# A two-layer graph network kernel: 70 early gathers, finishes by pairs of groups, one-hots made two groups ahead, and a share of the last weighted rows on GpSimd

## Chip, cores and metric

The kernel runs on one core of a Trainium2 chip, in a single launch. The metric is the device time of one execution in microseconds (us). Before the change the median of 10 runs is 2741.71 us (2734.19 to 2759.88). The core's engines are called PE (matmul), DVE (vector), ACT (scalar activation), POOL (GpSimd, which here issues the gathers) and SP (which issues the plain transfers).

## What is computed

The graph has N = 6250 nodes with 256 features (D) and 106,250 edges sorted by target, with self loops and two relations. Layer 0 sends along each edge a two-step message of the source node (a different weight for each relation), sums the messages by target, puts the sums through a gated update and a small network, adds the input and normalizes. Layer 1 is graph attention with 4 heads (H) of 64, followed by two more residual normalizations.

```python
S = feat[src]
for r in range(2):
    msgs = where(rel == r, relu(relu(S @ W_rel[r].T + b) @ W_rel[r].T + b), msgs)
agg = segment_sum(msgs, dst)
i, f, g, o = split(agg @ W_ih.T + b_ih + b_hh, 4)
hn = sigmoid(o) * tanh(sigmoid(i) * tanh(g))
x = layernorm(x + mlp(hn))
...
h = (x @ W).reshape(n, H, F)
e = leaky_relu(a_src[src] + a_dst[dst], 0.2)
ex = exp(e - segment_max(e, dst)[dst])
out = segment_sum(h[src] * (ex / (segment_sum(ex, dst)[dst] + 1e-16)), dst) + bias
y = relu(layernorm(out + x) * gamma + beta)
x = layernorm(x + y)
```

## The kernel before

**Tiling.** The edges other than self loops, in target order, are cut into TC = 782 tiles of 128. Seven tiles make a window (WT = 7, NW = 112 windows), two windows a group of 128 target nodes (NG = 56 groups of 14 tiles). A group's sums also use the first tile of the next group (GS = 15 tiles), since a tile's edges can run over the border. A segment sum over a group is a chain of matmuls into one PSUM bank: a one-hot matrix (edge by target) against the edge rows. `one_hot` builds a group's one-hots with three DVE instructions (L1835).

**Front.** The lists are made and both relations' messages are computed once for every source node, in blocks, and stored to the DRAM table `parts0`. After the block before BLOCK1 = 26 and the one before BLOCK2 = 39, POOL gathers the first edge rows early (L1606): `ahead_tiles` lists KEPT1 = 3 tiles of each of the first AHEAD_W = 12 windows for the first batch and KEPT2 = 2 for the second, 60 in all. The row buffers `G` are a ring of ten, seven tiles each, which the gathers of both layers use.

**Stage 0 (layer 0).** `order` goes through all other tiles, one gather a step (L1718, table `parts0`). LAG = 4 steps behind, `sum0` issues the matmul of that tile (L2178). When a group's sums are complete, DVE makes `kind` and `agg` from them (L1927, L1931), and for each four groups `update` runs gates, network and layer norm (the normalization's statistics end at L2062) and writes rows for layer 1. AHEAD_G are the groups whose windows had early gathers; their one-hots and first sums are issued ahead of the loop.

**Holds.** `Pace` remembers for every step the last DVE instruction traced so far. `Pace.hold` lets every fourth gather wait for the DVE instruction of the step `ahead` steps back: AHEAD0 = 6 steps in stage 0, AHEAD1 = 4 in stage 1, where an extra lead is given that falls from 42 steps to none over the first 250 tiles and grows again over the last 42. The instructions of an engine run in the order in which the program traces them; there is no other scheduling. `Steps` holds coroutines ("chains") that are advanced once a step; a `yield k` puts the rest off by k steps.

**Stage 1 (layer 1).** Groups are handled in 26 pairs, and the last four one by one (`pairs`). In order of a pair's life:

- `ahead`: for each group a DVE one-hot `ohT` (L2351), PE products `pn` that fetch the target's logits (L2365), and a DVE reduction `of` (L2369); also the segment borders `cut`, turned by PE and copied by ACT.
- `weights`: ACT has copied the logits from the gathered rows (L2642, L2651); PE turns them (L2392), DVE runs two scans (L2399, L2400), PE and ACT pass the ends between tiles (L2403 to 2405), DVE adds logits (L2406, L2407) and runs two more scans (L2409, L2410), PE turns back (L2415), DVE takes the maxima (L2418 to 2421), ACT exponentiates into PSUM `bank` (L2423).
- `weighted`: called by `sum1` for each window piece; makes the group's one-hots if they are not there, then `gw`, the rows times their weights (L2438 and L2444 on DVE, L2443 on ACT). A seven-tile piece is 128x1792 elements. Four `gw` buffers.
- `sum1`: the matmul of one tile into the group's PSUM sum `fps1`, of which there are two (L2564). With the first sum of an even group, SP loads `k3` (kept rows of two groups). With a group's last sum the chain `finish` starts.
- `finish` for one group: subtract, exponential (L2462, L2464, ACT L2465), denominator (L2468 to 2472), the own row and the sums (L2479, L2482), scaling and residual (L2485, L2486), `normed(0)` (L2494, L2495, ACT L2496/2497, DVE L2499, ACT L2502), weight, offset and relu (L2506 to 2508), `normed(1)`, store. The last group also moves rows by a matmul (L2518, L2526).

In the loop each step has one gather (from t = EARLY = 21 on; the first 21 are made between the stages), one or two calls of `sum1`, one `run.step()` and one `pace.passes()`.

Of the kernel before, what the change touches and what calls it, by code (L numbers as in the profile page):

```python
# [33 lines left out]
F32 = mybir.dt.float32  # L34
# [8 lines left out]
P = 128  # L43
# [3 lines left out]
H = 4  # L47
# [22 lines left out]
GS = 2 * WT + 1  # L70
LOW, MID = P // 2, (WT, WT + 3)
# [9 lines left out]
AHEAD_W = 12  # L81
# [7 lines left out]
AHEAD1 = WT - 3  # L89
# [1551 lines left out]
def fast(  # L1641
# [164 lines left out]
    rings = {("G", id(rowsp)): [list(bufs), -(-len(soon) // WT)]}  # L1806
# [43 lines left out]
    with (  # L1850
# [17 lines left out]
        b1c = l0w.tile([P, 1], F32, name="fb1c")  # L1868
        b2c = l0w.tile([P, 1], F32, name="fb2c")
# [337 lines left out]
        seven = bufs[len(soon) // WT].rearrange("p (j f) -> p j f", f=HA)  # L2207
        pace = Pace(len(soon))
        for n in range(len(soon), TC + LAG):
            if n < TC:  # L2210
# [17 lines left out]
                pace.hold(move, n, AHEAD0)  # L2228
# [30 lines left out]
    with (  # L2259
# [8 lines left out]
        vec_p = vps.tile([P, 2, D], F32, name="vec_p")  # L2268
        nc.scalar.copy(vec_p, vec)
# [9 lines left out]
        def complete(t):  # L2279
# [9 lines left out]
            more = ring(eps, [P, D + 2 * H], F32, "fps1", 2)[:, :HA]  # L2289
# [15 lines left out]
        def ahead(pair, box):  # L2305
# [25 lines left out]
            else:  # L2331
                o = pair[0] % 2 * GS * H
                n = ((len(pair) - 1) * GS + len(tiles_in(pair[-1])[1])) * H
                pc = ring(tps, [P, P + 1], F32, "turn", 2)
# [8 lines left out]
            yield 12 if len(pair) > 1 else 8  # L2343
            for i, g in enumerate(pair):
                halves = node2[g % 4]
                for h, ps in enumerate((low_s, high_s)):
                    nc.scalar.copy(
                        halves[ps, h, :], node3[ps, g, :, :].rearrange("p c a -> p (c a)")
                    )
                ohT = ring(ep, [P, MID[1], P], BF16, "ohT", 2)  # L2350
                nc.vector.tensor_scalar(  # L2351
                    ohT.rearrange("p j e -> p (j e)"), dB[:, i, :], iota_p, None, op0=OP.is_equal
                )
                yield 2
                n = len(tiles_in(g)[1])
                pn = ring(ops, [P, GS, 3, 2 * H], F32, "pn", 2)
# [20 lines left out]
        def weights(pair, box):  # L2377
# [13 lines left out]
            pe = ring(tps, [P, P + 1], F32, "turn", 2)[:, :P]  # L2391
# [10 lines left out]
            pd = ring(tps, [P, P + 1], F32, "turn", 2)[:, :P]  # L2402
# [11 lines left out]
            pm = ring(tps, [P, P + 1], F32, "turn", 2)[:, :P]  # L2414
# [16 lines left out]

        def weighted(g, w, o, n, of, ex, top):

            if g not in ohs:
                ohs[g] = ring(ep, [P, (2 * WT - 2) * LOW + 3 * P], F32, "oh1", 2)
                one_hot(ohs[g], g, slot, MID[1])
# [7 lines left out]
            made = nc.vector.tensor_mul(  # L2444
                gw[:, :, :D].rearrange("p j (h f) -> p j h f", h=H),
                of[:, :n, :D].rearrange("p j (h f) -> p j h f", h=H),
                ex[:, o : o + n, :, None].to_broadcast([P, n, H, F]),
# [7 lines left out]
        def finish(g, ps):  # L2455
            u = everyone
            n = u.stop
            at_w = lows_of([g])
            k3 = k3s[g // 2][:, g % 2, :, :]
            sm = ring(fp, [P, 4, H], F32, "sm", 3)  # L2460
            w_own, den = sm[u, 0, :], sm[u, 1, :]
            nc.vector.tensor_sub(w_own, loop[u, g, :], ps[u, HA:])  # L2462
# [7 lines left out]
                den, ps[u, D:HA], 1e-16, w_own, op0=OP.add, op1=OP.add  # L2470
            )
            nc.vector.reciprocal(den, den)
            yt = ring(fp, [P, D], F32, "fy", 3)
            y = yt[u, :]

            def heads(ap):
                return ap.rearrange("p (h f) -> p h f", h=H)

            nc.vector.tensor_mul(  # L2479
                heads(y), heads(k3[u, 2, :]), w_own[:, :, None].to_broadcast([n, H, F])  # L2480
            )
            nc.vector.tensor_add(y, y, ps[u, :D])  # L2482
            read.add(g)
            yield 1
            nc.vector.tensor_mul(heads(y), heads(y), den[:, :, None].to_broadcast([n, H, F]))  # L2485
            nc.vector.tensor_add(y, y, k3[u, 1, :])  # L2486
            yield 1
            mv = ring(fp, [P, 2, 2], F32, "fmv1", 3)
            rs = ring(fp, [P, 2, 2], F32, "frs1", 3)

            def normed(k):
                st = ring(fp, [P, nc.vector.BN_STATS_DIM], F32, "fst1", 3)
                r, m = rs[u, k, 0:1], rs[u, k, 1:2]
                nc.vector.bn_stats(st[u, :], y)  # L2494
                nc.vector.bn_aggr(mv[u, k, :], st[u, :])  # L2495
                nc.scalar.activation(r, mv[u, k, 1:2], AF.Ln, bias=eps_c[u])  # L2496
                nc.scalar.activation(r, r, AF.Exp, scale=-0.5)
                yield 2
                nc.vector.scalar_tensor_tensor(  # L2499
                    m, mv[u, k, 0:1], -1.0, r, op0=OP.mult, op1=OP.mult  # L2500
                )
                nc.scalar.activation(y, y, AF.Identity, bias=m, scale=r)  # L2502
# [3 lines left out]
            nc.vector.tensor_mul(y, y, vec_p[u, 0, :])  # L2506
            nc.vector.tensor_add(y, y, vec_p[u, 1, :])
            nc.vector.scalar_tensor_tensor(y, y, 0.0, k3[u, 0, :], op0=OP.max, op1=OP.add)
            yield 1
            yield from normed(1)  # L2510
            in_order(written, g)
            if g in at_w:
                nc.sync.dma_start(out[bass.ds(at_w[g], P), :], yt)
            results[g] = yt
            if g == NG - 1:
                moved = ring(eps, [P, D + 2 * H], F32, "fps1", 2)[:, :D]
                for q in range(2):
                    nc.tensor.matmul(  # L2518
                        moved,
# [202 lines left out]
```

## Time and profile before

| what | us |
|---|---|
| median of 10 runs | 2741.71 |
| profiled execution | 2747.18 |
| its span | 2745.3 |
| front, to the first gather of stage 0 | 257.8 |
| stage 0, to its last groups | 257 to 1422, POOL busy 712.5, DVE 372.9, PE 836.4 |
| change of stages | 1422 to 1500 |
| stage 1, to its last gather | 1500 to 2668, POOL busy 697.1, DVE 731.2, PE 526.7 |
| tail, without gathers | 2668 to 2745, DVE busy 52.1, PE 35.4 |
| L1718, 722 gathers of stage 0 | 693.5, 961 ns each |
| L1718, 761 gathers of stage 1 | 726.8, 955 ns each |
| L1606, 60 early gathers | 58.8 |
| L2444, 167 pieces `gw` | 249.0 |
| L2564, 1674 sums of stage 1 | 462.6 |

A line of a timeline has the start, the duration, engine, source line, operation, output and inputs, the count, and in brackets the idle time of that engine before it and what ended it. "Issue" there means that the profile shows no wait; "remote" and "another core or an unknown queue" that the releaser could not be found. A line of waits has the waiting instruction, what released it, the total in us, how often, and the longest. PE's ends in the records are modelled.

### The profile page before, as it was taken

The numbers are of one execution on the slowest core, as the hardware profiler recorded it, in microseconds if no ns is written. First come the engines' busy times: TensorE is split into PE (matmuls) and PEld (weight loads), VectorE is DVE, ScalarE is ACT, GpSimd is POOL, SyncE is SP. The second block draws the span as 40 slices with busy tenths as digits, with TensorE's granted clock in tenths as the row PEclk, the third lists the DMA queues.
The fourth block names the chain that finished last, engine by engine and source line by source line (L and its number), as shares of the span: only waits on it lengthen the run. The fifth ranks groups of instructions, "written<-read, shape, count | busy, mean of one in ns | idle before, by whom it ended". The sixth has DMA issues, their size and how long they took to land.

```text
span 2745.3 us, 21961 instructions
## 1 busy us (share of the span) xinstructions
PE 1624.4 (59%) x6113; PEld 877.7 (32%) x6113; DVE 1312.4 (48%) x3627; ACT 510.4 (19%) x1650; POOL 1538.5 (56%) x1610
## 2 busy tenths in 40 slices
PE   8956877657677677678744454453534435353444
PEld 5634433323333333234432322221322223122222
DVE  8642333223233232234322567575665757566557
ACT  3311121111211112112230111111111111111112
POOL 1534656556656666665545555555656566665650
PEclk9978988878888988789876766676767666666766
DMA  4334434434444344443424444434435354443440
GB/s 145 128 118 145 138 113 140 128 93 134 144 136 136 106 133 135 134 133 124 133 89 117 119 116 122 126 107 119 126 112 141 107 134 120 126 133 106 120 120 27
DMA packets 153969, 335.04 MB, mean 122 GB/s; under 512 B 37114, under 2 KB 74848, under 8 KB 153837
## 3 DMA queue, kind: packets, MB, share of 16 engines
q0 software_dynamic: 76048, 207.99, 27.3%
q1 hardware_dynamic: 75613, 122.50, 14.1%
q10 hardware_dynamic: 2176, 3.05, 0.3%
q8 instruction: 50, 0.82, 0.1%
q14 instruction: 82, 0.67, 0.1%
HBM read 280.89 MB, written 52.52 MB: 121 GB/s over the span
## 4 chain that ended last, share of the span: by engine, by line
PE 27%; DVE 25%; another core or an unknown queue 23%; issue 12%; ACT 5%; POOL 2%; DMA 2%; DVEq 0%; ACTq 0%; SPq 0%; POOLq 0%
PE fps L2178 10%; DVE gw L2444 6%; PE fpg L2009 5%; DVE oh L1835 3%; PE fps L2564 3%; POOL G L1718 2%; PE fpm L1572 2%; PE fpg L2095 1%; PE fph L1558 1%; DVE fst L2494 1%; DVE ohT L2351 1%; PE fps L2291 1%; PE fpg L2057 1%; DMA G<-parts,fidx 1%
## 5 line engine op out<-in xcount | busy, mean ns | idle before, releaser
L1718 POOL DMA_INDIRECT G<-rows,fidx x761 | 726.8, 955 | 489.7 <-issue 232.4
L1718 POOL DMA_INDIRECT G<-parts,fidx x722 | 693.5, 961 | 463.6 <-issue 202.5
L2178 PE MATMUL fps<-G,oh 128*64 128x257 f32 (+1 forms) x1674 | 499.8, 433 | 133.2 <-ACT G L2224 53.7
L2564 PE MATMUL fps<-gw,oh 128*64 128x264 f32 (+1 forms) x1674 | 462.6, 464 | 186.0 <-DVE gw L2444 165.7
L2178 PEld LDWEIGHTS fps<-G,oh 128*64 128x64 f32 (+1 forms) x1674 | 223.5, 164 | 382.3 <-issue 190.8
L2564 PEld LDWEIGHTS fps<-gw,oh 128*64 128x64 f32 (+1 forms) x1674 | 238.8, 175 | 331.2 <-DVE gw L2444 173.5
L2444 DVE TENSOR_TENSOR gw<-G,bank 128x1792 f32<-128x1792 f32 (+1 forms) x167 | 249.0, 1491 | 91.8 <-ACT gw L2443 62.2
L2009 PE MATMUL fpg<-faT,fWihT 128*128 128x512 f32 (+2 forms) x432 | 185.7, 557 | 7.0 <-issue 3.9
L1835 DVE TENSOR_TENSOR oh<-bank,fslot 128x448 f32<-128x448 f32 (+2 forms) x318 | 156.5, 547 | 10.2 <-ACT bank L2423 6.6
L2415 PE MATMUL turn<-fident,s 120*128 120x120 f32 (+2 forms) x30 | 13.3, 443 | 204.0 <-DVE s L2410 107.4
L2129 DVE COPY nd<-hr 128x4 f32<-128x4 f32 x53 | 9.4, 178 | 257.4 <-ACT hr L2101 197.9
L1558 PE MATMUL fph<-fxc,fWrT 128*128 128x512 f32 (+1 forms) x208 | 98.0, 621 | 46.3 <-issue 28.1
L1942 PE MATMUL fpg<-fident,agg 128*128 128x128 f32 x112 | 28.5, 344 | 127.6 <-DVE agg L1931 106.7
L2009 PEld LDWEIGHTS fpg<-faT,fWihT 128*128 128x128 f32 x432 | 77.5, 207 | 81.9 <-issue 73.7
L1572 PE MATMUL fpm<-fWrT,fhT 128*128 128x256 f32 x392 | 96.3, 398 | 11.9 <-DVE fms L1580 11.9
L1606 POOL DMA_INDIRECT G<-parts,fidx x60 | 58.8, 980 | 71.9 <-DMA parts<-fms 34.0
L2496 ACT ACTIVATE frs<-fmv,eps_c 128x1 f32<-128x1 f32 x112 | 33.0, 295 | 350.0 <-DVE gw L2438 87.3
L1927 DVE TENSOR_SCALAR kind<-fps 128x1 f32<-128x1 f32 x112 | 12.3, 150 | 167.8 <-PE fps L2178 78.2
L2502 ACT ACTIVATE fy<-fy,frs 128x256 f32<-128x256 f32 x112 | 66.8, 597 | 115.0 <-DVE frs L2499 76.6
L2462 DVE TENSOR_TENSOR sm<-loop,fps 128x4 f32<-128x4 f32 x56 | 8.5, 151 | 163.4 <-remote 153.7
L1572 PEld LDWEIGHTS fpm<-fWrT,fhT 128*128 128x128 f32 x392 | 76.3, 199 | 31.7 <-issue 12.8
L2095 PE MATMUL fpg<-Wx,fyT 128*128 128x264 f32 x224 | 77.2, 475 | 8.3 <-ACT fyT L2086 3.0
(351 smaller groups left out, 2044.4 us busy)
## 6 DMA issues: line engine op xcount, KB each, us to landing
kept<-keep SPq DMA_DIRECT2D x26, 768.0 KB
k<-kept SPq DMA_DIRECT2D x26, 768.0 KB
loop<-parts SPq DMA_DIRECT2D x55, 256.0 KB
parts<-fms SPq DMA_DIRECT2D x49, 256.0 KB
G<-parts,fidx POOLq DMA_INDIRECT x782
G<-rows,fidx POOLq DMA_INDIRECT x761
dB<-slots SPq DMA_DIRECT2D x26, 320.0 KB
out_dram<-fy SPq DMA_DIRECT2D x56, 128.0 KB
```

Source lines behind the costliest of these rows:

```text
L1558: nc.tensor.matmul(ph[:, :cols], WrT_s[:, r, k, m * P : (m + 1) * P], xc[:, k, :cols], start=(k == 0), stop=(k == 1),)
L1572: made = nc.tensor.matmul(pm[:, r, :], hT[:, r, k, j * P : (j + 1) * P], WrT_s[:, r, k, :], start=(k == 0), stop=(k == 1),)
L1606: nc.gpsimd.indirect_dma_start(out=of[:, n % WT, :D], out_offset=None, in_=parts0[: 2 * P * block, :], in_offset=bass.IndirectOffsetOnAxis ...
L1718: return nc.gpsimd.indirect_dma_start(out=to_tile, out_offset=None, in_=table, in_offset=bass.IndirectOffsetOnAxis(ap=idx, axis=0),)
L1835: nc.vector.tensor_tensor(to[:, o : o + len(js) * n].rearrange("p (j s) -> p j s", s=n), iota_s[:, None, cols].to_broadcast([P, len(js), n ...
L2009: nc.tensor.matmul(pg[:, :cols], WihT_s[:, k, c * P : (c + 1) * P], aT[:, k, :cols], start=(k == 0), stop=(k == 1),)
L2095: nc.tensor.matmul(ph[u, :], hs[i][:, k, u], Wx[:, k, :], start=(k == 0), stop=(k == 1))
L2178: nc.tensor.matmul(sums[g][to, :], ohj, got[t], start=begins, stop=ends)
L2444: made = nc.vector.tensor_mul(gw[:, :, :D].rearrange("p j (h f) -> p j h f", h=H), of[:, :n, :D].rearrange("p j (h f) -> p j h f", h=H), e ...
L2496: nc.scalar.activation(r, mv[u, k, 1:2], AF.Ln, bias=eps_c[u])
L2502: nc.scalar.activation(y, y, AF.Identity, bias=m, scale=r)
L2564: nc.tensor.matmul(sums[g][to, :], ohj, gw, start=begins, stop=ends)
```

## The change

- Early gathers: 14 windows in place of 12, so 42 + 28 = 70 tiles, which fill all ten row buffers. The ring then hands the buffers out in the order REFILL. In stage 0 the hold's lead becomes 6 + max(0, 56 − half of the gathers made).
- AHEAD1 is 6 in place of 4.
- PSUM of stage 1: the sums of a pair lie in one unit of two banks, with two units; the small turns share the halves of one bank; one `pn` buffer in place of two.
- `ahead`: one `ohT` instruction and one set of copies for both groups of a pair.
- `finish` takes a pair: the DVE instructions go over both groups at once (128x512 in place of 128x256; bn_stats and the ACT normalization stay by group), and it starts with the last sum of the pair's last group. The last four groups are still single. `k3` is loaded by `load_kept`, when the pair before the last is done with its own.
- One-hots: `hots(g + 2)` is issued as soon as group g's last sum is.
- From step TC on (after the last gather), every other seven-tile piece of `gw` is multiplied by GpSimd, which takes the weights from the copy of ACT in `gw` in place of PSUM.
- The two small bias columns of layer 0 share one tile.

```diff
+BANK = 512
...
-AHEAD_W = 12
+AHEAD_W = 14
+REFILL = (0, 6, 1, 2, 3, 7, 4, 5, 8, 9)
...
-AHEAD1 = WT - 3
+AHEAD1 = WT - 1
...
-    rings = {("G", id(rowsp)): [list(bufs), -(-len(soon) // WT)]}
+    rings = {("G", id(rowsp)): [[bufs[i] for i in REFILL], -(-len(soon) // WT)]}
...
-        seven = bufs[len(soon) // WT].rearrange("p (j f) -> p j f", f=HA)
+        seven = bufs[len(soon) // WT % len(bufs)].rearrange("p (j f) -> p j f", f=HA)
-                pace.hold(move, n, AHEAD0)
+                pace.hold(move, n, AHEAD0 + max(0, 8 * WT - (n - len(soon)) // 2))
...
+        turns = [tps.tile([P, 2, BANK // 2], F32, name="turn"), 0]
+
+        def half_of(turns):
+
+            turns[1] += 1
+            return turns[0][:, turns[1] % 2, : P + 1]
+
...
+            both = node2[pairs.index(pair) % 2]
+            for h, ps in enumerate((low_s, high_s)):
+                nc.scalar.copy(
+                    both[ps, : len(pair), h, :],
+                    node3[ps, pair[0] : pair[0] + len(pair), :, :].rearrange("p i c a -> p i (c a)"),
+                )
+            ohTs = ring(ep, [P, 2, MID[1], P], BF16, "ohT", 1)
+            nc.vector.tensor_scalar(
+                ohTs[:, : len(pair), :, :].rearrange("p i j e -> p i (j e)"),
+                dB,
+                iota_p,
+                None,
+                op0=OP.is_equal,
+            )
             for i, g in enumerate(pair):
-                halves = node2[g % 4]
-                for h, ps in enumerate((low_s, high_s)):
-                    nc.scalar.copy(
-                        halves[ps, h, :], node3[ps, g, :, :].rearrange("p c a -> p (c a)")
-                    )
-                ohT = ring(ep, [P, MID[1], P], BF16, "ohT", 2)
-                nc.vector.tensor_scalar(
-                    ohT.rearrange("p j e -> p (j e)"), dB[:, i, :], iota_p, None, op0=OP.is_equal
-                )
+                halves, ohT = both[:, i, :, :], ohTs[:, i, :, :]
                 yield 2
                 n = len(tiles_in(g)[1])
-                pn = ring(ops, [P, GS, 3, 2 * H], F32, "pn", 2)
+                pn = ring(ops, [P, GS, 3, 2 * H], F32, "pn", 1)
...
+        def hots(g):
+
+            ohs[g] = ring(ep, [P, (2 * WT - 2) * LOW + 3 * P], F32, "oh1", 2)
+            one_hot(ohs[g], g, slot, MID[1])
+
         def weighted(g, w, o, n, of, ex, top):
 
             if g not in ohs:
-                ohs[g] = ring(ep, [P, (2 * WT - 2) * LOW + 3 * P], F32, "oh1", 2)
-                one_hot(ohs[g], g, slot, MID[1])
+                hots(g)
...
-            made = nc.vector.tensor_mul(
+            by = nc.vector
+            if run.now >= TC and n > 1:
+                halves_done.append(g)
+                by = (nc.gpsimd, nc.vector)[len(halves_done) % 2]
+            made = by.tensor_mul(
                 gw[:, :, :D].rearrange("p j (h f) -> p j h f", h=H),
                 of[:, :n, :D].rearrange("p j (h f) -> p j h f", h=H),
-                ex[:, o : o + n, :, None].to_broadcast([P, n, H, F]),
+                (ex[:, o : o + n, :] if by is nc.vector else gw[:, :, D:HA])[:, :, :, None].to_broadcast(
+                    [P, n, H, F]
+                ),
...
-        def finish(g, ps):
-            u = everyone
-            n = u.stop
-            at_w = lows_of([g])
-            k3 = k3s[g // 2][:, g % 2, :, :]
-            sm = ring(fp, [P, 4, H], F32, "sm", 3)
-            w_own, den = sm[u, 0, :], sm[u, 1, :]
-            nc.vector.tensor_sub(w_own, loop[u, g, :], ps[u, HA:])
+        def finish(pair, ps):
+            n = len(pair)
+            at_w = lows_of(pair)
+            k3 = k3s[pair[0]][:, :n, :, :]
+            sm = ring(fp, [P, 2, 2, H], F32, "sm", 3)
+            w_own, den = sm[:, 0, :n, :], sm[:, 1, :n, :]
+            own = loop[:, pair[0] : pair[0] + n, :]
+            nc.vector.tensor_sub(w_own, own, ps[:, :n, HA : HA + H])
 
...
+            nc.vector.tensor_mul(heads(y), heads(k3[:, :, 2, :]), for_all(w_own))
+            nc.vector.tensor_add(y, y, ps[:, :n, :D])
+            read.add(pair[0])
+            yield n
+            nc.vector.tensor_mul(heads(y), heads(y), for_all(den))
+            nc.vector.tensor_add(y, y, k3[:, :, 1, :])
+            yield n
+            mv = ring(fp, [P, 2, 2, 2], F32, "fmv1", 3)
+            rs = ring(fp, [P, 2, 2, 2], F32, "frs1", 3)
 
             def normed(k):
-                st = ring(fp, [P, nc.vector.BN_STATS_DIM], F32, "fst1", 3)
-                r, m = rs[u, k, 0:1], rs[u, k, 1:2]
-                nc.vector.bn_stats(st[u, :], y)
-                nc.vector.bn_aggr(mv[u, k, :], st[u, :])
-                nc.scalar.activation(r, mv[u, k, 1:2], AF.Ln, bias=eps_c[u])
+                r, m = rs[:, k, 0, :n], rs[:, k, 1, :n]
+                for i in range(n):
+                    st = ring(fp, [P, nc.vector.BN_STATS_DIM], F32, "fst1", 4)
+                    nc.vector.bn_stats(st, y[:, i, :])
+                    nc.vector.bn_aggr(mv[:, k, i, :], st)
+                nc.scalar.activation(r, mv[:, k, :n, 1], AF.Ln, bias=eps_c)
                 nc.scalar.activation(r, r, AF.Exp, scale=-0.5)
...
+            for k, op in ((0, OP.mult), (1, OP.add)):
+                nc.vector.tensor_tensor(
+                    y, y, vec_p[:, k, None, :].to_broadcast([P, n, D]), op=op
+                )
+            nc.vector.scalar_tensor_tensor(y, y, 0.0, k3[:, :, 0, :], op0=OP.max, op1=OP.add)
+            used.add(pair[0])
+            load_kept()
+            yield n
...
+        def load_kept():
+
+            while wanted and (len(k3s) < 2 or pairs[len(k3s) - 2][0] in used):
+                pair = wanted.pop(0)
+                g = pair[0]
+                k3s[g] = ring(fp, [P, 2, 3, D], F32, "k3", 2)
+                of = k3s[g].rearrange("p i c f -> p i (c f)")
+                if len(pair) == 1:
+                    nc.sync.dma_start(of[:, 0, :], kept[g // 2, :, g % 2, :])
+                else:
+                    nc.sync.dma_start(of, kept[g // 2])
...
+            pair = pair_of[g]
+            k = pairs.index(pair)
+            if g not in sums and k >= 2 and pairs[k - 2][0] not in read:
                 return
             queue.pop(0)
             if g not in sums:
-                sums[g] = ring(eps, [P, D + 2 * H], F32, "fps1", 2)
+                if g == pair[0]:
+                    units[g] = ring(eps, [P, 2, BANK], F32, "fps1", 2)
+                    wanted.append(pair)
+                    load_kept()
+                sums[g] = units[pair[0]][:, pair.index(g), : D + 2 * H]
...
-            if left[g] == 0:
-                run.start(finish(g, sums[g]), 1)
-
-        node2 = [ep.tile([P, 2, 6 * H], BF16, name=f"node2_{i}") for i in range(4)]
+            if left[g] == 0 and g + 2 < NG:
+                hots(g + 2)
+            if left[g] == 0 and g == pair[-1]:
+                run.start(finish(pair, units[pair[0]]), 1)
```

## Prediction

> **What bounds the kernel.** I read the page first (busy shares, costliest groups), then the waits, the chain, busy time by stage, and at last the timelines of one pair of groups, of the front and of the tail. By stage: front 0–257 us, stage 0 to 1422, a change-over to 1500, stage 1 to 2668, tail to 2745. No engine is full, and gathering takes the same POOL time in both stages.
>
> ```profile
> PE 1624.4 (59%) x6113; PEld 877.7 (32%) x6113; DVE 1312.4 (48%) x3627; ACT 510.4 (19%) x1650; POOL 1538.5 (56%) x1610
> PE 27%; DVE 25%; another core or an unknown queue 23%; issue 12%; ACT 5%; POOL 2%; DMA 2%; DVEq 0%; ACTq 0%; SPq 0%; POOLq 0%
> ```
>
> A quarter of the chain is "unknown queue"; the waits say where:
>
> ```profile
> ACT ends L2405 <- remote: 218.1, 19, 12.5
> DVE sm L2462 <- remote: 153.7, 19, 10.4
> POOL G L1718 <- DVE fy L2508: 70.0, 17, 4.6
> ```
>
> Both "remote" waits are for PE (the pair's last sums, L2564, and L2403/2404). So DVE stands some 8 us, 19 times, for sums that PE has recorded as done. One pair, DVE:
>
> ```profile
> 2172.73 0.16 DVE L2462 TENSOR_TENSOR sm<-loop,fps 128x4 f32<-128x4 f32 x1 [6.39 <-remote]
> 2179.13 1.49 DVE L1835 TENSOR_TENSOR oh<-bank,fslot 128x448 f32<-128x448 f32 x3 [0.27 <-ACT bank L2423]
> 2180.92 2.02 DVE L2444 TENSOR_TENSOR gw<-G,bank 128x1792 f32<-128x1792 f32 x1 [0.21 <-issue]
> 2193.76 2.02 DVE L2444 TENSOR_TENSOR gw<-G,bank 128x1792 f32<-128x1792 f32 x1 [0.26 <-ACT gw L2443]
> 2214.64 0.16 DVE L2462 TENSOR_TENSOR sm<-loop,fps 128x4 f32<-128x4 f32 x1 [9.07 <-issue]
> ```
>
> POOL around the same release (I call it R, 2172.73):
>
> ```profile
> 2168.71 0.94 POOL L1718 DMA_INDIRECT G<-rows,fidx  x1 [0.30 <-issue]
> 2173.36 0.94 POOL L1718 DMA_INDIRECT G<-rows,fidx  x1 [3.71 <-DVE sm L2464]
> 2187.32 1.01 POOL L1718 DMA_INDIRECT G<-rows,fidx  x1 [4.26 <-DVE fy L2508]
> ```
>
> The reader should see three things. A pair costs 28 gathers of 1.25 us (0.95 + 0.30 issue) = 35.0 us, and its period, R to R, is 42 to 44 us through most of the stage, 43.3 typically. The 8.3 us between are three POOL pauses: 3.4 at R, 3.95 at L2508, 0.84 at L2499. And PE's sums come out late: the last one before R is recorded as ended at 2160.8, and R comes 3.0 us after POOL's last gather ended. In about half of the pairs POOL had stopped so, in the others R came 0.9 to 2.4 us after the last gather. Two early pairs (1620.6 to 1698), in which POOL had been held for 4.2 us in the middle of the late sums, took 38.5 us. So the stage is bounded by a loop: late sums hold DVE, DVE's step holds POOL, and POOL's pause lets the sums out.
>
> **The sum by parts.** The profiled execution took 2747.2 us (span 2745.3 and 1.9 around it), 5.5 above the median 2741.7. Differences are worked out in its rows, and set on the median.
>
> (1) *Ten more early gathers*, 6 in the first batch and 4 in the second.
>
> ```profile
> 169.81 0.95 POOL L1606 DMA_INDIRECT G<-parts,fidx  x1 [0.30 <-issue]
> 204.80 0.94 POOL L1606 DMA_INDIRECT G<-parts,fidx  x1 [34.05 <-DMA parts<-fms]
> 233.56 0.95 POOL L1606 DMA_INDIRECT G<-parts,fidx  x1 [0.30 <-issue]
> 257.75 0.94 POOL L1718 DMA_INDIRECT G<-parts,fidx  x1 [23.25 <-DMA parts<-fms]
> ```
>
> POOL is idle after both batches (34.0 and 23.3 us), so 7.5 and 5.0 us more fit. Stage 0 then gathers 712 rows in place of 722; at its steady 22.2 us a group (14 tiles, 1.59 each) that is 15.9 us. The same seen from PE: a seventh group is summed at the 6.9 us of the first ones (285.7, 292.3, 299.2, 305.9, 313.0) in place of 22.2. Against it: the chain of the front has unknown waits of PE of 9.8, 5.6 and 15.3 us just while the 60 early gathers run, 0.5 us a gather, so ten more cost up to 5. Also all ten buffers are now full, so the first gather of stage 0 waits until PE has summed a buffer, some 10 to 18 us after 257.75; it is covered by pre-gathered sums that last to 313 + 6.9, within which POOL from 270 still gathers 40 rows. The looser hold in stage 0 gives POOL a lead, worth nothing by itself while the rate behind it stays. Bounds −16 and +5; I take **−10**.
>
> (2) *Paired finish.* 128x256 costs 0.42 (pitch 0.455), 128x1280 1.49, 128x1792 2.02: 1.04 ns an element, so 128x512 is 0.69 (pitch 0.72). Seven wide steps save 7 × (0.91 − 0.72) = 1.3 us a pair, seven small ones of 0.15–0.18 (pitch 0.19) another 1.3, the joined ohT 0–0.2 (0.77 + 0.55 now). About 2.6 us of DVE a pair, but DVE is idle for longer than that before R, so by itself it buys nothing. What counts is the order. All of the finish now lies behind the pair's last sum: from the release R' come one-hots 1.49, logits 0.54, L2462/4 0.35, scans 1.0, L2468–2482 2.1, ohT 1.24, L2485/6 1.44, tops 1.15, four bn 1.25, first gw 2.3, sum 12.9 us to the first sum, against 10.3 now (2182.99). The last gw of the pair ends at R' + 27.3 by the same counting (now 2195.8, R + 23.1), though no finish stands between then and the next release.
>
> (3) *One-hots two groups ahead.* DVE makes them as soon as the last sum is issued, so it waits for that sum there, one instruction group earlier than L2462: 1.49 us move from before the first gw to right behind the release. In stage 1 that is nothing (same chain); ACT's L2405 and PE's scan ends lie under it. In the tail three sets of 1.45–1.48 (2681.91, 2703.44, 2719.99) leave the way to the first gw. Bounds −4.4 (all on the chain) and 0 (DVE waits for the sum instead): **−3**.
>
> (4) *AHEAD1 4 → 6.* Each fourth gather waits for the DVE step 6 back. I count steps around the release of groups 26 and 27, whose tiles are steps 364 to 391. DVE stuck at the one-hots (step 427) lets POOL run to gather 435, not 431; gather 436 needs step 430, done at R' + 5.5, and starts at R' + 6.1. Eight gathers later, R' + 16.1, gather 444 needs L2508 of the pair at R' + 18.6 to 19.3: a pause of 3.8. Later holds find their steps done (448 at R' + 25, step 442 about R' + 25; 452 and on, idle DVE). So period = 35.0 + 3.8 + (pause at 436), which is R' − (end of gather 435) + 5.8. If R' comes 1 to 3 us after gather 431's end, as in the rows now, it is 4 to 2 us ahead of 435: period 40.6 to 42.6. If it waits for POOL's stop plus 3.0: 35.0 + 3.8 + 8.8 = 47.6. Below lies 38.5, seen in two pairs. I take 42.5, near the upper end of the row-like case, because the pair's sums start and end later: −0.8 × 26 pairs = **−21**.
>
> (5) *GpSimd halves.* By the step count only the second half of each of the last two groups goes there. Now they are DVE's 2.02 us, each under PE's sums of the first half:
>
> ```profile
> 2707.41 2.02 DVE L2444 TENSOR_TENSOR gw<-G,bank 128x1792 f32<-128x1792 f32 x1
> 2707.22 6.60 PE L2564 MATMUL fps<-gw,oh 128*128 128x264 f32 x20 [6.89 <-DVE gw L2444]
> ```
>
> PE wants the second half some 3 to 4 us after it begins; GpSimd may start when ACT's copy is done, with DVE's first half. So it has about 5 us at the first group, 4.1 at the second (five tiles in the first half). No row shows such an operation on POOL. Its fill of 128x1152 took 1.05 us, so 1.6 is the low end; its iota of 128x84, the dearest per element, took 0.37, 4.4 ns, so 7.9 is the high end, some 3 to 4 us late in each group. DVE gets 2.02 us back early, which nothing waits for (PE's sums set the end). Bounds −2 and +7; nearest to the fill and to DVE's 2.02: **0**, with DVE's work beside it as cover.
>
> The Trainium skill speaks against this part: "GPSIMD Engine Reference", section 4.1, wants two-input elementwise work on VectorE, as GpSimd is about half as fast (section 3.1: 4497 ns for 2048 f32). An estimate from that page is 3.9 us a half, which would still just fit, so the sum would be the same. "SBUF — State Buffer", "SBUF: two separate sides", adds that a DVE instruction with two SBUF inputs and a GpSimd one that reads SBUF exclude each other; by that L2485–2508 would stand behind each half, up to 2 × 3.9 us, only some of it on the chain. No row of this trace shows either.
>
> (6) PSUM: one pair of banks for each pair's sums, turn in halves of one bank, one pn buffer. The second group's pn now waits for L2369 of the first, five steps earlier: nothing, hidden by DVE's order. k3's load on SP is issued with the pair's first sum, 28 us ahead of L2479.
>
> Sum: −10 − 3 − 21 + 0 = −34, so 2741.7 − 34 = **2708**.
>
> **Rivals.**
> *A: the period stays at 43.3.* For it: between 1698 and 2566 it hardly moved (42.7 to 44.8) though the holds changed much. Then −13: 2729. If the GpSimd half is late as well, or the early gathers stand in the way of the messages, 2740; that the one-hots do not really leave the chain belongs here.
> *B: the sums come out on time,* because the pause at gather 444 falls in the middle of the burst, as in the two early pairs: 38.5, −4.8 × 26 = −125, 2604; with part of the pairs 2650. Against it: 20 gathers back to back still follow that pause.
> *C: slower, gather 436's hold.* DVE stands at the one-hots until POOL stops, POOL now stops four gathers later (5.0 us), and is let go 5.5 us after the release. Period 47.6 in every pair: +4.3 × 26 = +112, 2841; with the mean half-way (45.3), +52 − 13: 2781. It decides from a period above 43.8. For it: in pairs at 1740–1870, where the hold was loose, R also came 3.0 us after POOL's stop, and the gather 3.8 later.
>
> **How the numbers follow.** Two kernels nearer than 0.3% (8 us) can't be told apart. Forecast 0.41 (own range 2685 to 2730), A 0.17, B 0.13, C 0.29. Faster: 0.40 of the forecast, 0.10 of A, all of B, 0.63; same: 0.01, 0.06 of A and 0.02 of C, 0.09; slower: 0.01 of A and 0.27 of C, 0.28. The range takes in C's half-way case and most of B's partial one: 2645 to 2790.
>
> **What would show it.** Early gathers: 42 and 28 rows of L1606, the second batch ending near 240, and the seventh group's kind (L1927) near 320. Order: first sum 12 to 13 us behind the release. Holds: POOL pauses behind L2482 (gather 436) and the paired L2508, both under 4 us, and a period of 40.6 to 43; a pause near 9 us would be C. One-hots: no L1835 between L2421 and the first gw. GpSimd: two POOL rows of L2444's kind under 4 us, with PE's 20 and 24 sums unbroken. The forecast is wrong if the release follows POOL's stop in every pair, or if stage 0 ends no earlier than before.

## Result: slower, and the profile after

The changed kernel takes 2794.0 us (median of 13 runs) beside 2742.8 before (46 runs): ratio 1.0187, interval 1.0167 to 1.0206, some 51 us slower. The forecast was 2708, the range 2645 to 2790. The profiled execution has a span of 2786.2, 40.9 above before, and by stage:

| stage | before | after | difference |
|---|---|---|---|
| to the last `kind` of stage 0 | 1422.6 | 1437.5 | +14.9 |
| from there to the last gather | 1244.8 | 1268.8 | +24.0 |
| tail | 77.9 | 79.9 | +2.0 |
| mean period of pairs 10 to 24, first sum to first sum | 43.5 | 45.1 | |

Lines of the changed kernel carry its own numbers. The gather is L1720 (L1718 before), the one-hots L1837 (L1835), the scans L2414 and L2415 (L2399, L2400), the scan ends L2420 (L2405), the rows' weights L2457 and L2467 (L2438, L2444), the sums L2610 (L2564). In `finish`, L2487 is L2462, L2508 is L2482 (the step that adds the sums), and L2540 is L2508.

The page's first two lines of the changed kernel (busy time by engine, then the chain by engine) against those shown before:

```profile
PE 1656.3 (59%) x6127; PEld 894.8 (32%) x6127; DVE 1244.8 (45%) x3235; ACT 468.8 (17%) x1474; POOL 1547.2 (56%) x1612
PE 25%; another core or an unknown queue 24%; DVE 24%; issue 10%; POOL 4%; ACT 4%; DMA 4%; ACTq 0%; SPq 0%; POOLq 0%; DVEq 0%
```

DVE's work fell by 67.6 us (1312.4 to 1244.8), about the 2.6 counted for each of 26 pairs, and the kernel was slower all the same. The unknown share of the chain stayed. The waits of the changed kernel (what waited, for what, us in total, times, longest):

```profile
ACT ends L2420 <- remote: 203.2, 11, 19.8
DVE s L2414 <- remote: 142.2, 13, 14.5
POOL G L1720 <- DVE gw L2457: 130.8, 38, 9.9
DVE oh L1837 <- remote: 104.1, 23, 15.2
POOL G L1720 <- DVE fy L2508: 74.4, 11, 8.0
```

DVE now stands at the one-hots for the late sums (predicted), and longer still at the scan L2414, which waits for PE's turned logits. POOL stands at steps of the new order. One pair, DVE's timeline (start, duration, line, in brackets the idle time before):

```profile
2471.21 1.09 DVE L1837 TENSOR_TENSOR oh<-bank,fslot 128x448 f32<-128x448 f32 x2 [6.84 <-remote]
2472.62 0.49 DVE L1837 TENSOR_TENSOR oh<-bank,fslot 128x320 f32<-128x320 f32 x1 [0.33 <-remote]
...
2475.97 0.69 DVE L2508 TENSOR_TENSOR fy<-fy,fps 128x512 f32<-128x512 f32 x1
```

POOL's timeline of the same pair and the one ahead of it:

```profile
2421.35 0.95 POOL L1720 DMA_INDIRECT G<-rows,fidx  x1 [0.30 <-issue]
2430.24 1.34 POOL L1720 DMA_INDIRECT G<-rows,fidx  x1 [7.94 <-DVE fy L2508]
...
2444.25 0.94 POOL L1720 DMA_INDIRECT G<-rows,fidx  x1 [3.85 <-DVE gw L2457]
...
2468.39 0.95 POOL L1720 DMA_INDIRECT G<-rows,fidx  x1 [0.30 <-issue]
2476.92 1.34 POOL L1720 DMA_INDIRECT G<-rows,fidx  x1 [7.59 <-DVE fy L2508]
```

This is rival C: POOL stops (2469.3), the one-hots, which need the sums, start 1.9 to 3.3 us behind that, and the held gather waits for the paired L2508 another 4 us. The two pauses are 7.6 to 7.9 and 3.85 (C had 8.8 and 3.8), and both pairs take 46.7 us.

Not all pairs are so. Of the fifteen pairs 10 to 24, eight are: their held gather waits 7.1 to 8.0 us, and from finish to finish they take 45.2 to 49.9, 47.2 in the mean (C said 47.6). The other seven take 42.5 to 44.4, 43.2 in the mean. In six of these DVE stands 12.0 to 14.5 us at the scan L2414, and the sums are there when it goes on; in all seven POOL pauses 2.1 to 4.6 us four gathers earlier. One of them, DVE's line and POOL's:

```profile
2377.48 0.42 DVE L2414 TENSOR_TENSOR_SCAN s<-cut,turn 120x128 f32<-120x128 f32 x1 [13.79 <-remote]
```

```profile
2378.62 0.94 POOL L1720 DMA_INDIRECT G<-rows,fidx  x1 [3.86 <-DVE s L2415]
```

The front (the last message step of DVE, then POOL's last early gather and first gather of stage 0), two views of the changed kernel:

```profile
266.10 0.69 DVE L1582 TENSOR_TENSOR fms<-fpm,fbrr 128x512 f32<-128x512 f32 x1 [1.03 <-PE fpm L1574]
```

```profile
245.10 0.94 POOL L1608 DMA_INDIRECT G<-parts,fidx  x1 [0.30 <-issue]
284.36 0.94 POOL L1720 DMA_INDIRECT G<-parts,fidx  x1 [38.32 <-DMA rows<-node]
```

The last message step was at 253.47 before: ten gathers of 1.25 us made it 12.6 later. The first gather of stage 0 is 26.6 later. 12.6 of that are these; the other 14.0 we put down to the full ring, in which PE must empty a buffer first (its first sums ran from 272.95 to 284.95). The profile names a DMA here, but the runs below bear the ring out: on the same kind of chip the first gather starts 4.3 us after the last message step in every run with 50 or 60 early gathers, and 18.3 to 18.5 in every run with 70.

### The profile page after: what moved, and what is told of

Its sections match the earlier page's. It is cut to its first block, busy times and chain, and to the rows that moved or that the text cites. A ratio compares the mean times of both kernels' runs of the same rounds, so it can differ in the third digit from the quotient of the medians.

```text
span 2786.2 us, 21374 instructions
## 1 busy us (share of the span) xinstructions
PE 1656.3 (59%) x6127; PEld 894.8 (32%) x6127; DVE 1244.8 (45%) x3235; ACT 468.8 (17%) x1474; POOL 1547.2 (56%) x1612
## 4 chain that ended last, share of the span: by engine, by line
PE 25%; another core or an unknown queue 24%; DVE 24%; issue 10%; POOL 4%; ACT 4%; DMA 4%; ACTq 0%; SPq 0%; POOLq 0%; DVEq 0%
PE fps L2180 9%; DVE gw L2467 7%; PE fpg L2011 5%; POOL G L1720 4%; PE fps L2610 4%; DMA G<-parts,fidx 3%; DVE oh L1837 3%; PE fpg L2097 2%; ACT fy L2530 1%; DVE fst L2521 1%; DVE fy L2537 1%; PE fpm L1574 1%; PE fps L2300 1%; PE fph L1560 1%
## 5 line engine op out<-in xcount | busy, mean ns | idle before, releaser
L1720 POOL DMA_INDIRECT G<-rows,fidx x761 | 731.2, 961 | 510.5 <-issue 208.8
L1720 POOL DMA_INDIRECT G<-parts,fidx x712 | 681.9, 958 | 478.5 <-issue 193.9
L2610 PE MATMUL fps<-gw,oh 128*64 128x264 f32 (+1 forms) x1674 | 485.2, 478 | 248.8 <-DVE gw L2467 168.1
L2180 PE MATMUL fps<-G,oh 128*64 128x257 f32 (+1 forms) x1674 | 511.7, 442 | 123.7 <-DMA G<-parts,fidx 42.8
L2610 PEld LDWEIGHTS fps<-gw,oh 128*64 128x64 f32 (+1 forms) x1674 | 249.0, 181 | 409.5 <-DVE gw L2467 181.2
L2180 PEld LDWEIGHTS fps<-G,oh 128*64 128x64 f32 (+1 forms) x1674 | 230.3, 169 | 375.4 <-issue 183.2
L2467 DVE TENSOR_TENSOR gw<-G,bank 128x1792 f32<-128x1792 f32 x165 | 244.6, 1482 | 128.3 <-ACT gw L2462 83.0
L1837 DVE TENSOR_TENSOR oh<-bank,fslot 128x448 f32<-128x448 f32 (+2 forms) x315 | 156.0, 547 | 114.6 <-remote 102.2
L2418 PE MATMUL turn<-s,toward 120*120 120x1 f32 (+2 forms) x60 | 14.3, 306 | 135.3 <-DVE s L2415 58.2
L2414 DVE TENSOR_TENSOR_SCAN s<-cut,turn 120x128 f32<-120x128 f32 (+2 forms) x30 | 12.5, 417 | 170.4 <-remote 142.2
```

Source lines behind the costliest of these rows:

```text
L1720: return nc.gpsimd.indirect_dma_start(out=to_tile, out_offset=None, in_=table, in_offset=bass.IndirectOffsetOnAxis(ap=idx, axis=0),)
L1837: nc.vector.tensor_tensor(to[:, o : o + len(js) * n].rearrange("p (j s) -> p j s", s=n), iota_s[:, None, cols].to_broadcast([P, len(js), n ...
L2180: nc.tensor.matmul(sums[g][to, :], ohj, got[t], start=begins, stop=ends)
L2467: made = by.tensor_mul(gw[:, :, :D].rearrange("p j (h f) -> p j h f", h=H), of[:, :n, :D].rearrange("p j (h f) -> p j h f", h=H), (ex[:, o ...
L2610: nc.tensor.matmul(sums[g][to, :], ohj, gw, start=begins, stop=ends)
```

## Two kinds of chip

The experiments fell on chips of two kinds. On the first (three chips), before takes 2707 to 2743 us; the result above is from such a one. On the second (two chips) it takes 2194 to 2196, the same instructions at nearly the same durations: a gather 0.95 us, L2444 2.02, a sum of L2564 0.46 and 0.47. Each chip was seen in one batch only, so "kind of chip" may as well be a condition of that batch. Two things differ in the records. One is the granted clock of PE, 0.84 beside 0.94 in stage 0 and 0.68 beside 0.72 in stage 1; no run tells whether that is a cause or comes of the waiting. The other is when a sum reaches its reader. The kernel before on the second kind, DVE's and then POOL's timeline at a release (the moment when DVE gets a pair's last sums):

```profile
1722.47 0.42 DVE L2399 TENSOR_TENSOR_SCAN s<-cut,turn 120x128 f32<-120x128 f32 x1
...
1724.47 0.16 DVE L2462 TENSOR_TENSOR sm<-loop,fps 128x4 f32<-128x4 f32 x1 [0.62 <-PE fps L2564]
```

```profile
1722.58 0.95 POOL L1718 DMA_INDIRECT G<-rows,fidx  x1 [0.30 <-issue]
1723.84 0.94 POOL L1718 DMA_INDIRECT G<-rows,fidx  x1 [0.30 <-DVE e L2406]
1725.08 0.95 POOL L1718 DMA_INDIRECT G<-rows,fidx  x1 [0.31 <-issue]
```

L2462 waits 0.62 us for PE (6 to 10 on the first kind), POOL never pauses in pairs 10 to 24, and the period is 35.7 us, of which 28 gathers of 1.25 are 35.0. So there stage 1 is bound by the gathers. Ratios below are against the kernel before on the same chip in the same batch; "late" means the first kind, "prompt" the second.

## Experiments

**1. 60 early gathers in the changed kernel** (late; `e1_60_early`).

```diff
-AHEAD_W = 14
+AHEAD_W = 12
-    rings = {("G", id(rowsp)): [[bufs[i] for i in REFILL], ...
+    rings = {("G", id(rowsp)): [list(bufs), ...
```

> The changed kernel with 60 early gathers in place of 70, all else kept. Theory F (front): an early gather holds the messages for its own 1.25 us, and with all ten row buffers full the first gather of stage 0 waits until PE has emptied one; together they make stage 0 end some 15 us late (last kind at 1437.5 in place of 1422.5). Then this gains about 15 us, 2794 to 2779, with the last message's DVE step back near 253 and the first gather of stage 0 near 258. Rival: the looser hold at the start of stage 0 is what costs; then the front comes back, but the end of stage 0 stays near 1437 and the time near 2794.

Ratio 1.018 (1.0143 to 1.0217). The front came back (first gather of stage 0 at 252.7, last `kind` at 1395.3), but the mean pair from 10 to 24 then took 45.6 us (45.1 in the change). Against the change's 1.0187 that is 2 us less, where 15 were expected. The stage gave them back at the same pause: of pairs 10 to 23, L2508 now held POOL in thirteen, beside ten. Why more pairs fall into it stays open; runs 6 and 7 show the 15 where the hold is another.

**2. AHEAD1 = 4 in the changed kernel** (late; `e2_ahead4`, and on another chip `e14_ahead4c`).

```diff
-AHEAD1 = WT - 1
+AHEAD1 = WT - 3
```

> The changed kernel with AHEAD1 back at 4. Theory H (hold): DVE stuck at the one-hots lets POOL run four gathers longer, sums come out only when POOL stops, and gather 436 waits 5 us behind the release; the period of pairs 10 to 26 (44.9 us in the changed kernel, 43.0 before) falls to 43 or less and the time by 30 us or more, to 2764 or less. Rival O (order): the finish and the one-hots between release and first sum set the period, not the hold; then the period stays at 44 to 46 and the time within 8 us of 2794.

> The changed kernel with AHEAD1 = 4 and its 70 early gathers. Where sums are late: 1.0038 again. Where none are: if the early gathers bring the gain of 0.5%, 0.993 to 0.996; if the longer hold brings it, by letting POOL go on while DVE is in the longer finish, 0.998 to 1.002.

1.0038 (1.0015 to 1.006) and 0.9993 (0.9963 to 1.0024): 41 and 53 us less than the change. Mean period of pairs 10 to 24 in the first: 42.4, beside 45.1. With the hold the largest part of the loss goes. In this run DVE's long waits for PE are gone too: DVE stands 4.3 to 5.7 us at L2414 in pairs 10 to 23, and goes on while POOL is issuing gathers.

**3. One-hots where they were** (late; `e3_no_hots`).

```diff
-            if left[g] == 0 and g + 2 < NG:
-                hots(g + 2)
```

> The changed kernel with the one-hots made where they were (just before the first weighted rows of a group). Theory H: the step at which DVE stands moves only from 427 to 428, so the same gather is held; period 44 to 46, time 2790 to 2800, and the tail some 3 us longer. Rival O: the wait of DVE for the sums at the one-hots, 102 us in 22 places, goes away and with it 30 us or more: 2764 or less.

1.0198 (1.0153 to 1.0243): no gain. Part of the wait at the one-hots moves to L2487 (50.6 us in 14), and a held gather still waits for the paired finish, now at L2540 (138.7 us in 20, up to 9.1).

**4. Only the early gathers, in the kernel before** (late; `e4_before_70`), **and 50 of them** (late; `e17_before_50`).

```diff
-AHEAD_W = 12
+AHEAD_W = 14        # 70; e17: 10, which is 50
```

The run with 70 also has the order of refilling and the joined bias tile that makes room; the lines above show the number alone.

> The kernel before with only the 70 early gathers added (with the order of refilling, and the joined bias tile that makes room for it). Theory F: the front gets 12 us longer, the first gather of stage 0 comes some 26 us later, and the whole is 10 to 18 us slower than before, 2753 to 2761. Rival: the early gathers are worth what was predicted, 10 us, and the front's delay in the changed kernel has another cause: 2733.

> The kernel before with 50 early gathers in place of 60. Theory F: an early gather costs its own time in the front where sums are late (10 more cost 15 us), so ten fewer gain 5 to 15 us there: 0.995 to 0.998. Rival: only the full ring costs, so ten fewer lose what a gather in stage 0 takes, 1.59 us each: 1.003 to 1.006. Where no sums are late, stage 0 gives back 1.2 us for each: 1.003 to 1.006.

70: 1.006 (1.0034 to 1.0085), 16 us slower. 50: 0.9968 (0.9939 to 0.9996), 9 us faster. On one chip (this run with 50, and run 7's two) the last message step is at 238.75, 252.50 and 263.43 us for 50, 60 and 70 gathers: 11 to 14 us for ten, about what POOL needs for them (12.5). One profile with 70, run 3's, has it at 255.59, so it scatters. On the prompt kind it is at 208.1 with 60 and 206.3 with 70: there the messages are not held.

**5. AHEAD1 = 6 alone, in the kernel before** (prompt: `e5_before_ahead6`, `e9_before_ahead6b`; late: `e12_before_ahead6c`).

```diff
-AHEAD1 = WT - 3
+AHEAD1 = WT - 1
```

> The kernel before with AHEAD1 = 6 alone. Theory H: POOL runs four gathers longer while DVE stands at the late sums, whatever the order of the finish; period 45 or more in place of 43, 20 to 50 us slower than before. Rival P: the longer hold hurts only together with the one-hots and the paired finish, which put 5.5 us between release and the step that gather 436 waits for; alone it moves the time by less than 8 us.

> The kernel before with AHEAD1 = 6 alone. Where sums are late, theory L: the held gather waits for L2482, 2.8 us behind the release, so 1.005 to 1.02. Rival: the hold costs only with the new order, 0.997 to 1.003. Where no sums are late: 0.9994 and 0.9996 again.

Prompt 0.9994 and 0.9996, both within 0.1% of 1: no pause is there to be moved. Late 0.9913 (0.989 to 0.9935), 24 us faster, which neither theory had. So the longer hold is not a cost by itself. POOL's pauses of this run, with the back-to-back gathers between them left out:

```profile
2239.39 1.04 POOL L1718 DMA_INDIRECT G<-rows,fidx  x1 [4.41 <-DVE e L2406]
...
2256.86 0.94 POOL L1718 DMA_INDIRECT G<-rows,fidx  x1 [2.68 <-DVE gw L2444]
...
2280.97 1.04 POOL L1718 DMA_INDIRECT G<-rows,fidx  x1 [4.41 <-DVE e L2406]
```

In this pair DVE's long wait stands at the scan L2399 (8.14 us, until 2238.25, 3.3 behind POOL's stop), and the held gather is let go by L2406, 0.8 us after that and ahead of the finish. The later pause falls among the sums. The pauses are 7.1 us, and the pair takes 41.6 (42.1 in the mean of pairs 10 to 24).

**6. 60 early gathers and AHEAD1 = 4**, the edits of 1 and 2 together (prompt: `e8_60_ahead4`, `e10_60_ahead4b`; late: `e13_60_ahead4c`), **and that without the early one-hots**, the edit of 3 as well (prompt; `e6_60_ahead4_nohots`).

> The changed kernel with 60 early gathers and AHEAD1 = 4, one-hots two ahead kept. Theory F and H together: the 15 to 20 us of the front and the 40 us of the hold both come off, 10 to 15 us faster than before (2693 to 2700 where before takes 2707). Rival: the two costs overlap (60 early gathers gained nothing with AHEAD1 = 6), then it stays at the 1.0038 of AHEAD1 = 4 alone, 2713 to 2722.

> The changed kernel with 60 early gathers and AHEAD1 = 4. Where sums are late, theory: both costs come off, 0.993 to 0.998. Rival: they overlap, 1.000 to 1.006. Where no sums are late: 0.999 again.

> The changed kernel with 60 early gathers, AHEAD1 = 4 and the one-hots where they were: what is left is the paired finish, the PSUM plan, the looser start of stage 0 and the GpSimd halves. Theory: the paired finish alone gains some 10 to 15 us in stage 1, 2690 to 2700 where before takes 2707. Rival: with nothing hiding them the one-hots stand before the first weighted rows and eat this, 2705 to 2715.

Late 0.994 (0.9915 to 0.9966), 15 us less than with 70 in the same batch (0.9993): the early gathers' cost, seen again. Prompt 0.999 and 0.9992. Without the early one-hots 1.016 (1.0134 to 1.0185) on the prompt kind: 38 us more, period 38.0 in place of 35.9. So there the paired finish needs them: without them POOL pauses 2.4 us a pair in place of 0.4.

**7. AHEAD1 = 8 in the changed kernel** (late; `e15_ahead8`, and with 60 early gathers `e16_60_ahead8`).

```diff
-AHEAD1 = WT - 1
+AHEAD1 = WT + 1
```

> The changed kernel with AHEAD1 = 8. Theory D (distance): gather 436 waits for L2489, 2.4 us behind the release, in place of the paired L2508 at 5.5, and gather 444 for step 436 in place of 438, so it passes; the pauses of a pair fall from 12 to 6 or 7 us, its period from 45 to 41 or 42, and the time by 60 to 90 us: 0.985 to 0.998 where sums are late. Rival S (stop): the further POOL may run, the later the sums come; then slower than the changed kernel, 1.019 or more. Where no sums are late: 0.994 to 0.996, as the changed kernel.

> The same with 60 early gathers. Theory D and the front's cost of 15 us: 0.98 to 0.993 where sums are late. Rival S: 1.018 or more. Where no sums are late, if the early gathers bring the gain: 0.998 to 1.001.

1.0021 (0.9992 to 1.0051), 45 us less than the change, where theory D had 60 to 90 and 0.985 to 0.998; and 0.9962 (0.9932 to 0.9992), 16 us less again, in place of 0.98 to 0.993. So D has the direction and not the size. POOL may run further and it is faster: rival S falls. POOL's pauses, the gathers between left out again:

```profile
2271.92 0.94 POOL L1720 DMA_INDIRECT G<-rows,fidx  x1 [4.94 <-DVE gw L2457]
...
2279.57 0.94 POOL L1720 DMA_INDIRECT G<-rows,fidx  x1 [2.96 <-ACT frs L2524]
...
2314.49 0.94 POOL L1720 DMA_INDIRECT G<-rows,fidx  x1 [4.80 <-DVE gw L2457]
```

There is no pause at the release any more, where theory D had one of 6; both lie among the sums. In the mean of pairs 10 to 24 POOL pauses 7.8 us a pair, beside 9.6 in the changed kernel. The release itself (one-hots at 2290.27) comes while POOL is issuing gathers back to back. The mean period of pairs 10 to 24 is 43.3 (45.1), less of a fall than the 41 to 42 expected; of pairs 3 to 10 it is 39.5 (42.4).

**8. The change itself, and a tighter hold, on the prompt kind** (`a_after`, `e11_before_ahead2`; `c_before` is the kernel before, for the stages).

```diff
-AHEAD1 = WT - 3
+AHEAD1 = WT - 5        # e11 alone, in the kernel before
```

> The kernel before itself, for its stages on the same chip as the other runs of this batch. Both theories: a ratio of 1, the last kind near 1395 and some 1313 us from there to the end on a chip on which it takes 2707.

> The changed kernel itself beside the kernel before on this chip. Runs so far fell on two kinds of chip: on one before takes 2707 to 2743 us and DVE waits for late sums, on the other 2194 and it does not. Theory L (late sums): the loss of 1.9% needs the late sums, as gather 436's hold and the fronts' delays feed on them; on the first kind 1.015 to 1.022, on the second 1.000 to 1.010. Rival: the loss is in the order of the work and shows on both, 1.015 or more.

> The kernel before with AHEAD1 = 6 alone, again. On the second kind of chip it was 0.9994. On the first kind theory L: the step that gather 436 waits for is only 2.8 us behind the release here (5.5 in the changed kernel), so a pair's period grows by 2 to 3 us less than there: 1.005 to 1.015. Rival: the hold matters only with the one-hots right behind the release: 0.997 to 1.003.

> The changed kernel with 60 early gathers and AHEAD1 = 4, again (0.999 on the second kind of chip). On the first kind theory: both costs come off and the paired finish with its early one-hots is left, 0.993 to 0.998. Rival: the two costs overlap, 1.000 to 1.006.

> The kernel before with AHEAD1 = 2: a tighter hold, whose gather waits for L2482, 2.8 us behind the release, in place of L2464. Theory L on the first kind of chip: what costs is the distance between the release and the step that the held gather waits for, so a tighter hold costs as a looser one does: pause at the release 6 in place of 3.4 us, period 45 to 46, 1.015 or more. Rival: what costs is how late POOL stops; then a tighter hold is no slower, 0.99 to 1.003.

The change is faster there: 0.9947 (0.9928 to 0.9966), 12 us. Its stage 0 ends at 1134.9, beside 1147.0 in the kernel before (1148.1 in run 5's on the same chip). That is not the early gathers alone. `e10_60_ahead4b`, on the same chip with 60 early gathers and AHEAD1 = 4, ends stage 0 at 1139.8, and takes 9.1 us more than the change from there to the last gather (1000.9 beside 991.8): in pairs 10 to 24 its POOL pauses 0.4 us a pair, the change's not at all. So in these profiles the ten gathers are worth 5 us, and with the paired finish the longer hold, which costs so much on the late kind, saves 9. AHEAD1 = 2 gives 1.0014 (1.0003 to 1.0026): nearly nothing, so it tells nothing of the late kind, where it was not run.

On the late kind the kernel before with AHEAD1 = 6 has the lowest ratio (0.9913; on the prompt kind 0.9994 and 0.9996), though its interval overlaps that of the change with 60 early gathers and AHEAD1 = 4 (0.994). On the prompt kind it is the change.

## Why the prediction was wrong

Taken apart in the order of runs 6, 2 and the change, the 51 us on the late kind are −16.5 for all but early gathers and hold (0.994), +14.5 for the ten gathers (0.9993) and +53 for AHEAD1 = 6 (1.0187). The order matters: with AHEAD1 = 6 in place the ten gathers cost only 2 (run 1).

- **The hold, −21: wrong in sign, and the largest.** The step that failed was "R' comes 1 to 3 us after gather 431's end, as in the rows now". In eight of the fifteen pairs 10 to 24 POOL stopped four gathers later, after the one that answers to 435, and the last one-hots came 1.6 to 3.7 us after that: the sums came four gathers later too. These pairs took 47.2 us in the mean where the forecast had 40.6 to 42.6 and C 47.6. In the other seven POOL did stop where it does now, as gather 432 waited 2.1 to 4.6 us for the scans; the forecast let it pass. They took 43.2. The prediction had bounds for both, took the first for every pair, and the mean of 45.1 is near C's half-way 45.3. The row that spoke for C was named in the text: pairs at 1740 to 1870, in which R followed POOL's stop under a loose hold too.
- **Not only the hold.** In the kernel before, the longer hold gains 24 us (run 5), so the loss is from hold and order together: the longer hold puts the held gather behind the paired L2508. The text had this as "5.5 us after the release", and runs 2 and 7 bear it out: with another step in that place 41 to 53 us are back.
- **Early gathers, −10: wrong in sign.** Measured +16 alone (run 4). The step that failed is the price of 0.5 us a gather, read from the unknown waits of the chain (30.7 us over 60 gathers). It is 1.3 (12.6 us for ten): those waits are only a part of what the messages lose. In the kernel before, DVE made three message steps during the second batch (204.8 to 234.5), at 205.82, 215.00 and 221.28. The upper bound of +5 was too low for that reason. The gain on the other side is real: group 7 follows group 6 after 7.2 us in run 4, beside 16.0 before.
- **Full ring, costed at nothing.** The wait came as described (14.0 us), but its cover did not hold: group 0 needs late tiles too, and its `kind` went from 276.2 to 295.7. The lag grew to 46 us at the sixth group, was back at 17.6 by the thirteenth, and 14.9 at the end.
- **Paired finish:** DVE's saving was about as counted. The first sum comes 14.6 us behind the first one-hot (2437.05 − 2422.41) where 12.9 were counted; 2.4 of that are the third one-hot's own wait, so the work itself is 12.2. That it buys nothing by itself is not shown: no late run has it alone, and what is left of the change without early gathers and hold gains 16 us there (run 6), and 2, which is within the noise, on the prompt kind.
- **One-hots, −3:** none stands before the first gw in the tail, but the tail is 2.0 longer, so the gain did not show. That they are nothing in stage 1 was right on the late kind (run 3) and wrong on the prompt (38 us, run 6).
- **GpSimd halves, 0: right.** 3.19 us each, within 1.6 and 7.9 and under the prediction's estimate of 3.9 from "GPSIMD Engine Reference"; PE's 20 and 24 sums ran unbroken in 5.51 and 6.81.

## What to carry to other kernels

When a wait has no releaser in the profile, find out what ends it before moving what it hangs on. In the kernel before and in the change the long waits mostly ended 1 to 4 us after POOL's own stop, but in runs 2 and 7 shorter ones ended with POOL running, so the stop is not shown to be what ends them. What a hold cost hung on the step that the held gather waited for, not on how loose it was. Work put beside a stage that stands still for unknown reasons is not free because its engine is idle; measure what it delays by doing more and less of it. And run a change on more than one chip where such waits are: here its sign turned (1.0187 and 0.9947).

## What the runs showed of the hardware

A DVE instruction with two SBUF inputs did not get past a GpSimd multiply that reads SBUF. The changed kernel's tail, POOL's view, then DVE's:

```profile
2750.11 3.19 POOL L2467 TENSOR_TENSOR gw<-G,gw 128x1792 f32<-128x1792 f32 x1 [42.87 <-ACT gw L2462]
2763.47 3.19 POOL L2467 TENSOR_TENSOR gw<-G,gw 128x1792 f32<-128x1792 f32 x1 [10.18 <-ACT gw L2462]
```

```profile
2750.69 0.88 DVE L2537 TENSOR_TENSOR fy<-fy,vec_p 128x256 f32<-128x256 f32 x2 [0.72 <-ACT fy L2530]
2751.60 1.97 DVE L2540 SCALAR_TENSOR_TENSOR fy<-fy,k 128x256 f32<-128x256 f32 x1
...
2763.64 3.29 DVE L2512 TENSOR_TENSOR fy<-fy,k 128x256 f32<-128x256 f32 x1
```

L2540 and L2512 take 0.42 us in this form elsewhere; here they end 0.27 us behind GpSimd's end (2753.57 to 2753.30, 2766.93 to 2766.66), and the change's profile on the prompt kind has 1.98 and 3.29 us in the same two places. The Trainium skill, "SBUF — State Buffer", "SBUF: two separate sides", says of the port pair that DVE and GpSimd share: whoever comes second waits for the whole instruction. The trace agrees. L2537, with its second input in PSUM, ran at full speed at the same time (two in 0.88). The 4.4 us cost next to nothing here: the last group's finish (L2487) began 0.93 us behind PE's last sum, beside 0.76 before.

That one program at nearly the same instruction times takes 2194 us on one chip and 2743 on another was not expected. The records differ in the granted clock and in when PE's work reaches its readers while POOL issues gathers back to back (0.62 us of DVE's waiting at L2462, beside 6 to 10). What makes it late on some chips was not found.
